# Second attention of a fused network: the order of scores and products inside a round, the product cut in halves, and the order of four PSUM banks

## The chip, the cores and the metric

The program runs on one core of one Trainium2 chip, as one launch. The metric is the device time of the launch in microseconds (us), as the median of several runs; lower is better.

## The reference, cut to what matters

The network has two layers; x has shape (2, 1024, 256) in float32. The change touches only the second attention (`L0_attn_b`), which adds its output to x:

```python
NH, NKV = 16, 4                       # 16 query heads, 4 heads of keys and values
HD = C // NH                          # 16
q = _rope((x @ Wq).reshape(b, t, NH, HD).transpose(0, 2, 1, 3))
k = _rope((x @ Wk).reshape(b, t, NKV, HD).transpose(0, 2, 1, 3))
v = (x @ Wv).reshape(b, t, NKV, HD).transpose(0, 2, 1, 3)
k, v = jnp.repeat(k, 4, axis=1), jnp.repeat(v, 4, axis=1)
scores = jnp.einsum('bhqd,bhkd->bhqk', q, k) / sqrt(HD)
scores = jnp.where(causal, scores, finfo.min)
y = jnp.einsum('bhqk,bhkd->bhqd', jax.nn.softmax(scores, axis=-1), v)
return y.transpose(0, 2, 1, 3).reshape(b, t, c) @ Wproj
```

## The kernel before, in words

All arithmetic is in float32. The stage treats four chunks of 512 query rows, one after the other: batch 0 rows 0 to 511 (c = 0) and 512 to 1023 (c = 1), then batch 1 likewise. Within a chunk it goes through t = 0 to 3; one t stands for four query heads, one for each head g of keys and values, and the four g lie at partitions 32g, so that four matmuls of 32 rows can run side by side in the array.

For each t the scores are computed twice.

- `highest` (L891, matmuls at L898, called Q below) makes scores by query rows: for 128 queries and up to 512 keys, one PSUM bank for each g. VectorE reduces each bank to the negated row maximum (L906 where the diagonal has to be masked, L911 elsewhere) and writes it beside the queries. A list `quads` holds these steps, 16 for a chunk with c = 0 and 32 for a chunk with c = 1, over (t, 128 queries, up to 512 keys). With c = 1 the eight steps of one t have 512, 128, 512, 256, 512, 384, 512 and 512 keys.
- `turn` (L913) transposes the queries of one t with their maxima into `qm` (matmuls at L919, copied out by ScalarE at L921). With c = 1 VectorE first merges two maxima (L916).
- `round_.scores` (L928, matmuls at L933, called S) makes the same scores by keys: 128 keys by m queries, again one bank for each g. ScalarE takes the exponential of each bank into `pr` (L938); GpSimd zeroes what lies above the diagonal (L942).
- `round_.weigh` (L947, matmuls at L952, called W) multiplies `pr` with v into the bank `py`, which is accumulated over the key blocks kb. After the last block `divide_by_sums` (L997) runs on VectorE: a transpose (L1002), a reciprocal (L1004), a product (L1008) and, for every second t, one more transpose (L1013).

With c = 0 the four blocks of a t have m = 512, 384, 256, 128; with c = 1 the eight have 512 five times, then 384, 256, 128. A matmul in float32 leaves two rows in the profile.

Seven PSUM banks (tag "sc") go round in the order in which tiles are asked for; the eighth is `py`. A matmul into a tile waits until the instruction that last read that bank is done.

The order of PE, VectorE, ScalarE and GpSimd is the order of issue in the source (`in_order`). The loop over n at L824 issues one step of `quads`, the first `piece` of the list for this n, W of the round issued two steps earlier, S of the round that lags ten steps behind `quads`, then `turn` where one is due, then the other pieces. Pieces are the work for the next chunk (transposes, projection at L327 with its rope on VectorE, `turn_keys` L882, `turn_queries` L888) and the output products of the chunk before (L965, added to x at L970). They are spread over the first three chunks; the last chunk has only the output pieces of the one before.

Of the kernel before, what the change touches and what calls it, by code (L numbers as in the profile page):

```python
# [27 lines left out]
def interleave(a, b):  # L28

    ia = ib = 0  # L30
    while ia < len(a) or ib < len(b):
        if ib >= len(b) or (ia < len(a) and ia * len(b) <= ib * len(a)):
            a[ia]()
            ia += 1
        else:
            b[ib]()
            ib += 1
# [102 lines left out]
class Net:  # L140
# [625 lines left out]
    def attn_b(self, w, wo, cos, sin, ffn):  # L766

        nc, tc = self.nc, self.tc
        lead = 10
        with ExitStack() as ctx:
            big = ctx.enter_context(tc.tile_pool(name="b_big", bufs=1))
            work = ctx.enter_context(tc.tile_pool(name="b_work", bufs=2))
            ps = ctx.enter_context(tc.tile_pool(name="b_ps", bufs=1, space=PSUM))


            qpad = [big.tile([P, 4, 4, 4, 32], F32, name=f"q_pad{j}") for j in range(2)]
            kpad = [big.tile([P, 4, 32], F32, name=f"k_pad{j}") for j in range(2)]
            for p in qpad + kpad:
                nc.gpsimd.memset(p, 0.0)
            for p in kpad:
                nc.gpsimd.memset(p[:, :, 16:17], 1.0)

            mask = big.tile([P, 512], BF16, name="mask")
            nc.gpsimd.memset(mask[:, 0 : 512 - P], 0.0)  # L790
            nc.gpsimd.tensor_copy(mask[:, 512 - P :], self.neg)
            ctx.enter_context(self.in_order())
            pools = (ps, big, work, w, wo, cos, sin, kpad, mask)
            chunks = []
            for b in range(B):
                kT = big.tile([P, T], F32, tag="kT", name="kT", bufs=2)
                v = big.tile([P, NB, 4, 32], F32, tag="v", name="v", bufs=2)
                nc.gpsimd.memset(v[:, :, :, 16:32], 1.0)
                chunks += [self.attn_b_chunk(pools, b, c, kT, v, qpad[c]) for c in range(2)]

            def bank(name):
                return ps.tile([P, 512], F32, tag="sc", name=name, bufs=7)

            owed = [step for _, step in self.ffn0_pieces(work, bank, 12, *ffn)]
            interleave(owed, chunks[0].inputs)
            quads, rounds, turns, fill = [], [], {}, {}

            def add(n, step):
                fill.setdefault(n, []).append(step)

            for n, chunk in enumerate(chunks):
                at = len(quads)
                size = len(chunk.quads)
                inputs = chunks[n + 1].inputs if n + 1 < len(chunks) else []
                for m, steps in enumerate(self.spread([1.0] * (size - 1), inputs)):
                    for step in steps:
                        add(at + m, step)
                for j, step in enumerate(chunk.outputs):
                    add(at + size + lead + 3 + j, step)
                for t in range(4):  # L820
                    turns[at + (t + 1) * size // 4] = chunk.turns[t]
                quads += chunk.quads
                rounds += chunk.rounds
            for n in range(max(fill) + 1):  # L824
                pieces = fill.get(n, [])
                here, last = (
                    rounds[n - lead - j] if 0 <= n - lead - j < len(rounds) else None
                    for j in (0, 2)
                )
                if n < len(quads):  # L830
                    quads[n]()
                for piece in pieces[:1]:
                    piece()
                if last:
                    last.weigh()
                if here:
                    here.scores()
                if n in turns:
                    turns[n]()
                for piece in pieces[1:]:  # L840
                    piece()

    def attn_b_chunk(self, pools, b, c, kT, v, qk):
# [5 lines left out]
        end = 4 * c + 3  # L849

        def psum(name):
            return ps.tile([P, 512], F32, tag="sc", name=name, bufs=7)
# [38 lines left out]
        def highest(t, j, lo):  # L891

            i = 4 * c + j
            n = min(512, (i + 1) * P - lo)
            tiles = [psum("s1") for _ in range(4)]
            for g in range(4):
                rows = slice(32 * g, 32 * g + 32)
                nc.tensor.matmul(  # L898
                    tiles[g][:, 0:n], shared["qT"][rows, t, j * P : (j + 1) * P],
                    kT[rows, lo : lo + n], start=True, stop=True,  # L900
                )
            for g in range(4):
                out = qk[:, j, t, g, HD : HD + 1] if lo == 0 else shared["nm2"][:, t, j, g : g + 1]
                if lo + n == (i + 1) * P:
                    masked = work.tile([P, 512], F32, tag="masked", name="masked")
                    nc.vector.tensor_tensor_reduce(  # L906
                        masked[:, 0:n], tiles[g][:, 0:n], mask[:, 512 - n :], -1.0, 3e38,
                        ALU.add, ALU.min, out,
                    )
                else:  # L910
                    nc.vector.tensor_reduce(out, tiles[g][:, 0:n], AX.X, ALU.max, negate=True)  # L911
# [11 lines left out]
        def round_(t, kb):  # L923
            own = type("round", (), {})()
            q0 = max(512 * c, kb * P)
            m, off = 512 * (c + 1) - q0, q0 - 512 * c

            def scores():  # L928
                pr = own.pr = work.tile([P, 4, 512], F32, tag="pr", name="pr", bufs=4)
                tiles = [psum("s2") for _ in range(4)]  # L930
                for g in range(4):
                    rows = slice(32 * g, 32 * g + 32)
                    nc.tensor.matmul(  # L933
                        tiles[g][:, 0:m], kT[rows, kb * P : (kb + 1) * P],
                        shared["qm"][t][rows, off:512], start=True, stop=True,
                    )
                for g in range(4):
                    nc.scalar.activation(pr[:, g, off:512], tiles[g][:, 0:m], AF.Exp, scale=0.25)  # L938
                if kb >= 4 * c:

                    d = pr[:, :, off : off + P]
                    nc.gpsimd.affine_select(  # L942
                        out=d, in_=d, compare_op=ALU.is_ge, fill=0.0, base=0,
                        pattern=[[0, 4], [1, P]], channel_multiplier=-1,
                    )

            def weigh():  # L947
                if kb == 0:
                    shared["py"] = ps.tile([P, 512], F32, tag="py", name="py")
                py = shared["py"]  # L950
                for g in range(4):
                    nc.tensor.matmul(  # L952
                        py[32 * g : 32 * g + 32, off:512], v[:, kb, g, :], own.pr[:, g, off:512],
                        start=(kb == 0), stop=(kb == end),
                    )
                if kb == end:
                    self.divide_by_sums(work, py, shared["yT"], t)

            own.scores, own.weigh = scores, weigh
            return own  # L960

        def output(j):
# [9 lines left out]
        chunk = type("chunk", (), {})()  # L972
        chunk.quads = [
            lambda t=t, j=j, lo=lo: highest(t, j, lo)
            for t in range(4) for j in range(4) for lo in range(0, (4 * c + j + 1) * P, 512)
        ]
# [1324 lines left out]
```

## Time and profile before

| What | Value |
|---|---|
| Median of 3 runs | 2863.79 us (2859.41 to 2870.02) |
| Profiled execution: span from first to last instruction | 2865.0 us |
| Mean granted TensorE clock of the core | 0.932 |
| Busy share of the span | PE 88%, PEld 54%, DVE 71%, ACT 46%, POOL 37% |
| Matmul rows at L898, L933, L952 | 768 each |
| First Q, first S, first W, last W (start) | 504.3, 535.1, 541.7 and 873.0 us |

The page gives no time of the profiled execution other than its span, which is 1.2 us above the median of the runs. PE is the matmul engine, PEld its weight loads, DVE VectorE, ACT ScalarE, POOL GpSimd. In a timeline row the columns are the start and the length in us, the engine, the source line, the operation, output and inputs, the shape, how many instructions were merged into the row, and in brackets the idle time of the engine before it and what ended it. Ends of matmuls are modelled; starts are recorded. A group of four matmuls that runs side by side shows as x8.

### The profile page before, as it was taken

The numbers are of one execution on the slowest core, as the hardware profiler recorded it, in microseconds if no ns is written. First come the engines' busy times: TensorE is split into PE (matmuls) and PEld (weight loads), VectorE is DVE, ScalarE is ACT, GpSimd is POOL, SyncE is SP. The second block draws the span as 40 slices with busy tenths as digits, with TensorE's granted clock in tenths as the row PEclk, the third lists the DMA queues.
The fourth block names the chain that finished last, engine by engine and source line by source line (L and its number), as shares of the span: only waits on it lengthen the run. The fifth ranks groups of instructions, "written<-read, shape, count | busy, mean of one in ns | idle before, by whom it ended". The sixth has DMA issues, their size and how long they took to land.

```text
span 2865.0 us, 66910 instructions
## 1 busy us (share of the span) xinstructions
PE 2520.3 (88%) x26384; PEld 1555.7 (54%) x26384; DVE 2028.8 (71%) x6762; ACT 1330.0 (46%) x2800; POOL 1063.2 (37%) x1600
## 2 busy tenths in 40 slices
PE   6999998999998877988888888888868999989888
PEld 2334334444433444655655555555646777767777
DVE  5777774766767968679786878788656767767651
ACT  2686870345454435676666675757611222212110
POOL 3444242211115757567554665565510001101000
PEclk9999998999999966999998999899978999999898
DMA  4000000000001100000000000000011110101100
GB/s 122 1 1 1 1 1 1 1 1 1 1 1 45 45 1 1 1 1 1 1 1 1 1 1 1 1 1 1 1 35 25 25 25 22 21 15 35 25 9 15
DMA packets 61978, 35.37 MB, mean 12 GB/s; under 512 B 43216, under 2 KB 58080, under 8 KB 61664
## 3 DMA queue, kind: packets, MB, share of 16 engines
q1 hardware_dynamic: 59472, 29.49, 4.0%
q8 instruction: 207, 3.39, 0.5%
q10 hardware_dynamic: 2192, 1.61, 0.2%
q14 instruction: 107, 0.88, 0.1%
HBM read 22.68 MB, written 8.39 MB: 11 GB/s over the span
## 4 chain that ended last, share of the span: by engine, by line
PE 38%; DVE 14%; POOL 4%; ACT 4%; issue 3%; SPq 1%; DMA 1%; ACTq 0%; POOLq 0%; DVEq 0%
PE ph L1521 6%; PE pg L2115 5%; PE e L1273 4%; DVE p L1284 4%; PE pu L2115 4%; PE po L2133 3%; PE dT L1345 3%; PE po L1540 2%; DVE p L1323 2%; POOL p L1331 1%; PE py L1375 1%; POOL p L1311 1%; ACT p L1294 1%; PE kh L1726 1%; PE pq L327 1%
## 5 line engine op out<-in xcount | busy, mean ns | idle before, releaser
L1294 ACT ACTIVATE p<-p,nm 128x128 f32<-128x128 f32 (+7 forms) x512 | 391.2, 769 | 79.8 <-DVE nm L1290 42.2
L1284 DVE CUSTOM_DVE_ANT_0 p<-e,mask 128x512 f32<-128x512 f32 (+3 forms) x768 | 382.3, 553 | 61.4 <-PE e L1273 61.0
L1331 POOL TENSOR_SCALAR p<-p,md 128x128 f32<-128x128 f32 (+7 forms) x256 | 241.6, 948 | 180.0 <-DVE md L1323 162.6
L1359 ACT ACTIVATE pT<-dT 128x384 f32<-128x384 f32 (+3 forms) x384 | 176.6, 487 | 203.2 <-PE dT L1345 202.2
L1273 PE MATMUL e<-kT,qT 32*128 32x512 f32 (+3 forms) x1536 | 230.5, 580 | 43.7 <-DVE nm L1284 40.8
L1345 PE MATMUL dT<-ident,p 128*128 128x128 f32 x1152 | 197.1, 297 | 65.2 <-POOL p L1331 36.6
L1323 DVE CUSTOM_DVE_ANT_0 p<-p,nrs 128x128 f32<-128x128 f32 (+7 forms) x256 | 221.3, 890 | 25.9 <-POOL p L1315 25.7
L938 ACT ACTIVATE pr<-s 128x512 f32<-128x512 f32 (+3 forms) x384 | 157.3, 496 | 162.9 <-PE s L933 154.2
L1311 POOL TENSOR_SCALAR p<-p,ra,neg_lam 128x128 f32<-128x128 f32 (+7 forms) x256 | 219.5, 857 | 9.2
L1345 PEld LDWEIGHTS dT<-ident,p 128*128 128x128 f32 x1152 | 138.0, 149 | 153.5 <-POOL p L1331 67.9
L654 ACT ACTIVATE pr<-s 128x1024 f32<-128x1024 f32 (+1 forms) x192 | 145.4, 813 | 125.6 <-PE s L648 77.4
L2115 PE MATMUL pg<-xT,gate 128*128 128x256 f32 x576 | 158.6, 423 | 4.6 <-ACT inter L2120 3.4
L898 PE MATMUL s<-kT,qT 32*128 32x512 f32 (+3 forms) x768 | 155.0, 518 | 4.3 <-DVE q_pad L906 2.5
L906 DVE CUSTOM_DVE_ANT_0 masked<-s,mask 128x128 f32<-128x128 f32 (+3 forms) x256 | 110.7, 487 | 59.1 <-PE s L898 59.0
L659 ACT ACTIVATE pr<-pr 128x1024 f32<-128x1024 f32 (+1 forms) x192 | 152.2, 852 | 0.0
L2133 PE MATMUL po<-down,inter 128*128 128x256 f32 x576 | 144.2, 395 | 5.8 <-DVE inter L2125 5.8
L1273 PEld LDWEIGHTS e<-kT,qT 32*128 32x128 f32 x1536 | 84.8, 203 | 116.3 <-DVE nm L1284 72.7
L662 POOL TENSOR_SCALAR_AFFINE_SELECT pr<-pr 128x256 f32<-128x256 f32 x128 | 89.3, 716 | 152.1 <-ACT pr L659 55.1
L2115 PE MATMUL pu<-xT,up 128*128 128x256 f32 x576 | 141.3, 389 | 0.8 <-ACT inter L2120 0.7
L2120 ACT ACTIVATE inter<-pg 128x512 f32<-128x512 f32 x72 | 43.0, 597 | 195.7 <-PE pg L2115 195.7
L2115 PEld LDWEIGHTS pg<-xT,gate 128*128 128x128 f32 x576 | 116.5, 209 | 27.1 <-issue 4.7
L300 POOL TENSOR_SCALAR ln_xn<-x,ln_mv,rsq_y 128x256 f32<-128x256 f32 x128 | 89.8, 710 | 108.1 <-DVE rsq_y L279 88.8
(295 smaller groups left out, 5344.1 us busy)
## 6 DMA issues: line engine op xcount, KB each, us to landing
uk_d<-uk SPq DMA_DIRECT2D x128, 32.0 KB, 1.9
r<-uk_d SPq DMA_DIRECT2D x8, 512.0 KB, 3.5
x<-in_L_attn_a_X SPq DMA_DIRECT2D x4, 512.0 KB, 6.7
qh_d<-qh SPq DMA_DIRECT2D x8, 256.0 KB, 2.1
o<-qh_d SPq DMA_DIRECT2D x128, 16.0 KB, 1.8
out<-x SPq DMA_DIRECT2D x4, 512.0 KB, 4.4
w<-in_L_ffn_W2T SPq DMA_DIRECT2D x1, 1024.0 KB, 7.7
pk<-in_L_ffn_gate_packed SPq DMA_DIRECT2D x8, 128.0 KB, 2.4
```

Of the source, the lines that this page charges most:

```text
L938: nc.scalar.activation(pr[:, g, off:512], tiles[g][:, 0:m], AF.Exp, scale=0.25)
L1273: nc.tensor.matmul(own.tiles[h][:, a, 0 : hi - lo], made["q"][r : r + 32, a, t, :], kT[r : r + 32, a, lo:hi], start=True, stop=True,)
L1284: nc.vector.tensor_tensor_reduce(own.p[h][a][:, lo:hi], own.tiles[h][:, a, 0 : hi - lo], neg_row[:, T - nk + lo : T - nk + hi], -1.0, 3e38 ...
L1294: nc.scalar.activation(own.p[h][a], own.p[h][a], AF.Exp, bias=own.nm[:, h, a : a + 1], scale=-1.0, accum_out=own.sm[:, h, a : a + 1],)
L1311: nc.gpsimd.tensor_scalar(p1, p1, own.ra[:, h : h + 1], nlam[:, head : head + 1], ALU.mult, ALU.mult)
L1323: nc.vector.tensor_tensor_reduce(p0, p0, p1, own.nrs[:, h : h + 1], 3e38, ALU.add, ALU.min, own.md[:, h : h + 1],)
L1331: nc.gpsimd.tensor_scalar(p0, p0, -1.0, own.md[:, h : h + 1], ALU.mult, ALU.add)
L1345: nc.tensor.transpose(dT[:, n, :], own.p[h][0][:, kb * P : (kb + 1) * P], self.ident)
L1359: nc.scalar.activation(shared[t, s + h][:, lo:hi, :], own.dT[h, part][:, 0 : hi - lo, :], AF.Exp)
L1521: nc.tensor.matmul(ph[:, j, :], w[:, kc, m * P : (m + 1) * P], f.xT[:, kc, :], start=(kc == 0), stop=(kc == 1),)
L2115: nc.tensor.matmul(ph[:, j, :], m_[:, kc, m * P : (m + 1) * P], f.xT[:, kc, :], start=(kc == 0), stop=(kc == 1),)
L2133: nc.tensor.matmul(f.po[:, b], inter[m // 2][:, m % 2, b * P : (b + 1) * P], wd[:, m % 2, (m // 2) * C : (m // 2 + 1) * C], start=(b == m ...
```

## The change

Inside one step n of the loop the order becomes S, the first half of W, Q, the first piece, the second half of W, `turn`, the other pieces. W is cut in the middle of its query columns where it has at least 256 of them (80 of the 96 rounds); a W of 128 columns is issued whole at the place of the first half. The four matmuls of S and of Q are issued from g = 3 down to g = 0, while their banks are still asked for, and read, from g = 0 up.

```diff
+                if here:
+                    here.scores()
+                if last:
+                    last.weigh(0)
                 if n < len(quads):
                     quads[n]()
                 for piece in pieces[:1]:
                     piece()
                 if last:
-                    last.weigh()
-                if here:
-                    here.scores()
+                    last.weigh(1)
                 if n in turns:
                     turns[n]()
...
             tiles = [psum("s1") for _ in range(4)]
-            for g in range(4):
+            for g in reversed(range(4)):
...
                 tiles = [psum("s2") for _ in range(4)]
-                for g in range(4):
+                for g in reversed(range(4)):
...
-            def weigh():
-                if kb == 0:
+            cuts = [off, (off + 512) // 2, 512] if m >= 256 else [off, 512]
+
+            def weigh(part):
+
+                if part + 1 >= len(cuts):
+                    return
+                if kb == part == 0:
                     shared["py"] = ps.tile([P, 512], F32, tag="py", name="py")
                 py = shared["py"]
+                at = slice(*cuts[part : part + 2])
                 for g in range(4):
                     nc.tensor.matmul(
-                        py[32 * g : 32 * g + 32, off:512], v[:, kb, g, :], own.pr[:, g, off:512],
-                        start=(kb == 0), stop=(kb == end),
-                    )
-                if kb == end:
+                        py[32 * g : 32 * g + 32, at], v[:, kb, g, :], own.pr[:, g, at],
+                        start=(kb == part == 0), stop=(kb == end), skip_group_check=True,
+                    )
+                if kb == end and part + 2 == len(cuts):
                     self.divide_by_sums(work, py, shared["yT"], t)
```

## The prediction

> **What bounds the kernel now.** I read the page first, for the groups of the three products, then the windows over the stage, then the timeline of single rounds. Units are us.
>
> ```profile
> L938 ACT ACTIVATE pr<-s 128x512 f32<-128x512 f32 (+3 forms) x384 | 157.3, 496 | 162.9 <-PE s L933 154.2
> ...
> L898 PE MATMUL s<-kT,qT 32*128 32x512 f32 (+3 forms) x768 | 155.0, 518 | 4.3 <-DVE q_pad L906 2.5
> L906 DVE CUSTOM_DVE_ANT_0 masked<-s,mask 128x128 f32<-128x128 f32 (+3 forms) x256 | 110.7, 487 | 59.1 <-PE s L898 59.0
> ```
> ```profile
> 530.00:870.00 340.00, 333.84 (x2426) 142.38 (x2428) 228.24 (x743) 170.71 (x413) 54.82 (x96) 1.00 0.00 1
> ```
> In the window (columns: length, then busy PE, PEld, DVE, ACT, POOL, clock) PE is busy 334 of 340, DVE 228, ACT 171. Exponentials and reductions wait for PE; PE waits for nobody. So the stage is bound by PE's order. But PE is not full, as one round of full width shows:
>
> ```profile
> 814.53 1.07 PE L952 MATMUL py<-pr,v 128*32 128x512 f32 x8
> ...
> 815.53 1.14 PE L933 MATMUL s<-qmT,kT 32*128 32x512 f32 x8
> ...
> 816.49 2.03 PE L898 MATMUL s<-kT,qT 32*128 32x512 f32 x8
> ...
> 816.75 2.06 ACT L938 ACTIVATE pr<-s 128x512 f32<-128x512 f32 x4 [1.64 <-PE s L933]
> 817.39 0.29 PEld L898 LDWEIGHTS s<-kT,qT 32*128 32x128 f32 x2 [0.70 <-ACT pr L938]
> 817.54 2.48 DVE L911 TENSOR_REDUCE q_pad<-s 128x1 f32<-128x512 f32 x4 [1.92 <-PE s L898]
> 818.45 0.16 PEld L952 LDWEIGHTS py<-pr,v 128*32 128x32 f32 x8 [0.76 <-issue]
> ```
> From start to start W takes 1.00, S 0.96 and Q 1.96. Q is twice S because S holds four of the seven banks: three of Q's matmuls go together, the fourth waits for the bank of the first exponential (817.39) and runs alone until 818.45, 1.06. The round is 3.92.
>
> **What the change removes.** With the banks in reverse the first matmul issued waits for the bank that comes free last, and all four then go side by side. Such a group followed by another kind of matmul costs 1.07 (861.86 to 862.93):
>
> ```profile
> 861.86 1.14 PE L933 MATMUL s<-qmT,kT 32*128 32x512 f32 x8
> ...
> 862.93 0.33 PEld L952 LDWEIGHTS py<-pr,v 128*32 128x32 f32 x8 [0.76 <-issue]
> ```
>
> **What it adds on PE.** A half of W is 256 wide and costs 0.57 (the W of 256 columns at 804.49 is followed by S at 805.06), two halves 1.14 instead of 1.00; S, now followed by W, 1.07 instead of 0.96. PE's own work in a full round is 1.07 + 0.57 + 1.07 + 0.57 = 3.28, 0.64 less than now. The 640 further matmul rows (80 split rounds, 8 rows each) lie in these prices.
>
> **What it adds in waits.** Only 7 banks stand against 8 in a round, so each group waits for the one before it.
> - Q waits for S's first exponential. S starts at 815.53, the exponential at 816.75, its bank is free at 817.39: 1.86 (1.81 at 819.44 to 821.25); I take 1.85. PE has S and half of W to do until then, 1.64.
> - The next S needs the bank of Q's first reduction. Q's four end 1.2 after their start, as S's do, a reduction takes 2.48/4 = 0.62 and the release 0.05, together 1.9. PE has Q and half of W, 1.64.
> A full round without a piece becomes 1.85 + 1.9 = 3.75: the 0.64 shrinks to 0.17. Of narrow groups these sums are 1.45, 1.15, 0.85 (S of 384, 256, 128) and 1.55, 1.2, 0.86 (Q), from the same kind of rows; before, narrow rounds simply cost PE less.
>
> Two VectorE steps change places too.
> - **The divide.** W's last block stood behind Q; now its L1002, L1004 and L1008 come ahead of Q's reductions in VectorE's queue, and the next S waits for the first of those:
>
> ```profile
> 808.05 0.72 DVE L1002 STREAM_TRANSPOSE turned<-py 128x512 f32<-128x512 f32 x1
> ...
> 808.80 0.25 DVE L1004 RECIPROCAL rec<-turned 128x16 f32<-128x16 f32 x1
> ...
> 809.09 0.42 DVE L1008 TENSOR_TENSOR pair<-turned,rec 128x256 f32<-128x256 f32 x1
> ```
>  That is 1.46, and 0.71 more for every second t.
> - **The turn.** With c = 1, L916 stands in VectorE's queue behind all four reductions of this step's Q, and PE stands at the transposes behind it:
>
> ```profile
> 824.05 1.86 PE L898 MATMUL s<-kT,qT 32*128 32x512 f32 x8
> ...
> 825.10 2.48 DVE L911 TENSOR_REDUCE q_pad<-s 128x1 f32<-128x512 f32 x4 [1.11 <-PE s L898]
> 825.84 1.06 PE L952 MATMUL py<-pr,v 128*32 128x512 f32 x8
> ...
> 826.83 0.71 PE L933 MATMUL s<-qmT,kT 32*128 32x256 f32 x8
> ...
> 827.50 0.17 DVE L916 TENSOR_TENSOR q_pad<-q_pad,nm 128x16 f32<-128x16 f32 x1
> ...
> 827.73 0.66 PE L919 MATMUL qm_ps<-ident,q_pad 128*128 128x128 f32 x4 [0.19 <-DVE q_pad L916]
> ```
>  From Q to the turn it is 3.68, now covered by Q, W and S. In the new order only Q and half of W are left, 1.64, and Q ends later since all four go together: 1.2 + 2.48 + 0.25 = 3.95, so PE stands still for 2.3. Queued behind it are S and with it ScalarE.
>
> **The sum, one t of eight rounds (c = 1, no pieces).** Key blocks 0 to 7 meet Q of 512, 256, 512, 384, 512, 512, 512, 128 keys. New: 3.75; block 1 has the divide (VectorE busy with the last Q until 1.8, divide to 3.25 or 4.0, first reduction 0.42, so 4.1 on the mean); 3.75; 1.85 + 1.55 = 3.4; 3.75; block 5 waits for the fourth reduction of the Q before at 1.85, then 1.9, 3.75; block 6 with the turn 1.85 + 3.95 + 0.59 = 6.4; block 7 0.85 + 0.86 = 1.7. Together 30.6. Before: 804.49 to 831.43, the starts of W of 256, 26.94. So +3.7 a cycle; its first six rounds alone, 22.5 against 21.15, +1.35.
> - Steps 26 to 47 and 74 to 95 are of this kind, two cycles and six rounds each: 2 x (7.4 + 1.35) = +17.5. Pieces give back. An output piece of 1.06 fills waits: 1.85 + 1.07 + 1.06 + 0.57 = 4.55 against 4.98 now, and beside a turn it is hidden whole; a small one (0.26) takes a bank, so that S waits for one more reduction, +0.36. Over 8 output, 4 projection and some 9 small pieces I count -8. Net +9.5.
> - Steps 16 to 25 and 64 to 73 (Q of c = 1 with S of 512, 384, 256, 128): by the same sums steps 64 to 73 take 4.0, 2.05, 3.75, 4.1, 3.05, 3.35, 3.75, 4.4, 6.4 and 1.7, together 36.5, with two divides and one turn, against 30.5 now (from the Q that starts at 741.25 to the one at 771.74), less 0.7 for one output piece that fills a wait. The short S no longer shorten a round. Some +5 each, +10.
> - Steps 48 to 63 (short Q, a piece in nearly every round): where S has 512 and Q 256 beside a projection, 1.85 + 0.65 + 1.49 + 0.57 = 4.55 against 4.76, where a small piece stands beside a wide Q up to 0.4 more; on the whole -1. Steps 0 to 15 (no W yet, or pieces throughout) and the end without Q: 0, within 3.
> Sum +18.5. On the profiled 2865.0 that is 2883.5; on the median, 1.2 lower, 2882.
>
> Bounds: 0.1 in each of the 84 rounds' waits is 8 either way. The six wide turns are 9 to 14, or nothing if the merge comes sooner. The clock is a risk from above: waits of VectorE already lowered it where Q runs alone, but not in the loose end of the stage.
>
> ```profile
> 510.00:515.00 5.00, 3.84 (x10) 1.72 (x10) 4.62 (x22) 0.00 (x0) 1.47 (x4) 0.50 0.00 0
> ...
> 860.00:876.00 16.00, 12.07 (x108) 3.52 (x105) 2.11 (x4) 10.45 (x26) 2.55 (x4) 1.00 0.01 2
> ```
> The new rounds (3.28 of 3.75 busy, the turn aside) are nearer to the second row, so I price the clock at 0; a half clock of 3.4 at each of 8 turns would be +14 if PE bound it, and twice that for 6.8.
>
> The Trainium skill speaks against such an order: "TensorE: Matmul & The Clock Gate", in "A second HAM failure mode: psum-queue depth-cycling", says that PE waiting briefly between groups as PSUM banks cycle lets the clock swing between half and full. The row at 860, with its waits and a clock of 1.00, does not show it; by the page's figure of half the clock the whole of the 340 would be open to a far larger loss, as an estimate 340/0.75 - 340 = 113 us if it swung half the time with PE as the bound.
>
> **The rivals.**
> - *Faster: PE stays the bound.* If the half products and pieces cover the waits for banks at S and Q, a full round is 3.28. It decides at the next S: if its bank is free 1.64 after Q instead of 1.9. About 50 full Q at 0.64 and the narrow ones for a little: -35, 2829. For it: PE idles 6 of 340 today. Against: it idles so little because single matmuls fill the very waits.
> - *No change: the turn is covered.* The six wide turns stand in the sum with about 1.5 each after what pieces hide, 9, and ten divides beside a Q of c = 1 with 0.9, 9. If S's earlier place lets VectorE run ahead so that both are covered, nothing is left: about 2864. For it: VectorE is busy only 228 of 340. Against: its queue is in order, and the rows above stand behind Q whatever its idle time.
> - *Slower still: the clock.* Holes of 2.3 at the turns drop the clock: +14 to +27 on top, about 2903. For it the row at 510, against it the row at 860, which has holes of up to 1.8.
> - *It does not do what it says.* Q still runs in two pieces, for its banks come free one by one: then only the added 0.36 a split round is left, 80 x 0.36 = +29, 2893.
>
> **How the numbers follow.** A measurement tells about 0.5%, 14 us, from no change. Chances: my sum 0.50 (0.84 of it over 2878), clock 0.14, two pieces 0.08, covered turn 0.18, PE the bound 0.10. Slower 0.42 + 0.14 + 0.08 = 0.64; same 0.08 + 0.18 = 0.26; faster 0.10. The likeliest is my sum, 2882. For 8 in 10 the range leaves out most of the PE rival and the far end of the clock: 2853 to 2910.
>
> **What would show it.** L952 has 1408 rows. Q of 512 runs as one group of four, about 1.07 to the next group. PE's idle time names DVE q_pad L906 and L911 before S, ACT pr L938 before Q, and about 2.3 before L919 behind L916 in six turns. PE's busy time in the stage falls by 30 or more while its span grows. The forecast is wrong if PE stays over 95% busy, if Q still shows a lone matmul, or if the turns wait under 1.

## The result: 1.7% slower, more than twice what was forecast

| | before | after |
|---|---|---|
| Median of the runs, us | 2861.6 (2857.96 to 2870.02) | 2913.76 (2910.82 to 2918.24) |
| Ratio to before, 95% interval | 1 | **1.0173** (1.0152 to 1.0194) |
| Span of the profiled execution, us | 2865.0 | 2909.2 |
| Mean granted TensorE clock of the span | 0.932 | 0.924 |

The direction was right, the size was not: 2882 was forecast, with 2910 as the upper end. In the profiled executions the changed kernel is 44.2 us longer, and the forecast sum was +18.5. All of it arises in the stage of the second attention; the first S starts at 535.3 in the one profile and at 535.1 in the other.

### The profile page after: what moved, and what is told of

It reads as the page before. It is cut to its first block, busy times and chain, and to the rows that moved or that the text cites. A ratio compares the mean times of both kernels' runs of the same rounds, so it can differ in the third digit from the quotient of the medians.

```text
span 2909.2 us, 68108 instructions
## 1 busy us (share of the span) xinstructions
PE 2549.1 (88%) x27024; PEld 1572.3 (54%) x27024; DVE 2028.9 (70%) x6762; ACT 1329.8 (46%) x2800; POOL 1056.9 (36%) x1600
## 4 chain that ended last, share of the span: by engine, by line
PE 37%; DVE 15%; POOL 4%; ACT 4%; issue 3%; SPq 0%; DMA 0%; POOLq 0%; DVEq 0%; ACTq 0%
PE ph L1529 5%; PE pg L2123 4%; PE e L1281 4%; DVE p L1292 4%; PE pu L2123 4%; PE po L2141 3%; PE dT L1353 3%; PE po L1548 2%; DVE p L1331 2%; PE py L1383 1%; POOL p L1339 1%; ACT p L1302 1%; POOL p L1319 1%; PE kh L1734 1%; PE pq L327 1%
## 5 line engine op out<-in xcount | busy, mean ns | idle before, releaser
L944 POOL TENSOR_SCALAR_AFFINE_SELECT pr<-pr 128x512 f32<-128x512 f32 x64 | 41.4, 646 | 252.5 <-ACT pr L940 162.8
L900 PE MATMUL s<-kT,qT 32*128 32x512 f32 (+3 forms) x768 | 130.6, 571 | 1.7 <-DVE q_pad L908 1.5
L2123 PEld LDWEIGHTS pg<-xT,gate 128*128 128x128 f32 x576 | 115.6, 208 | 28.2 <-issue 6.9
```

The costliest lines, as they stand in the source:

```text
L2123: nc.tensor.matmul(ph[:, j, :], m_[:, kc, m * P : (m + 1) * P], f.xT[:, kc, :], start=(kc == 0), stop=(kc == 1),)
```

## The profile after

The same window view as before, now over the longer stage. Its columns are length, busy PE, PEld, DVE, ACT and POOL, then the granted clock.

```profile
530.00:917.00 387.00, 366.58 (x3062) 161.40 (x3060) 231.57 (x759) 172.77 (x416) 54.91 (x97) 0.93 0.01 1
```

Before, the clock of this stage was 1.00 and PE was idle for about 6 us. Now the clock is 0.93 and PE is idle for 20. VectorE and ScalarE are busy for about as long as before (232 and 173 us, then 228 and 171), so no work was added there. The groups of instructions of this stage (busy time, mean ns, idle time ahead of them and what ended it):

```profile
L940 ACT ACTIVATE pr<-s 128x512 f32<-128x512 f32 (+3 forms) x384 | 156.9, 499 | 162.8 <-PE s L935 162.7
L900 PE MATMUL s<-kT,qT 32*128 32x512 f32 (+3 forms) x768 | 130.6, 571 | 1.7 <-DVE q_pad L908 1.5
L935 PE MATMUL s<-qmT,kT 32*128 32x512 f32 (+3 forms) x768 | 124.2, 563 | 7.2 <-DVE nm L908 5.3 <-DVE q_pad L908 1.8
L960 PE MATMUL py<-pr,v 128*32 128x256 f32 (+2 forms) x1408 | 103.2, 372 | 0.4 <-POOL pr L944 0.4
L921 PE MATMUL qm_ps<-ident,q_pad 128*128 128x128 f32 x64 | 11.3, 301 | 13.1 <-DVE q_pad L918 13.1
```

Q (L900) fell from 155.0 to 130.6 us of PE. The last line shows the one large new wait: 13.1 us ahead of the turn's transposes, for the merge of the two maxima. The second and third show that S and Q still wait for almost nothing in the records. That doesn't mean that they run as wanted, as the timeline of a full round shows:

```profile
859.85 1.28 PE L935 MATMUL s<-qmT,kT 32*128 32x512 f32 x8
861.05 0.64 PE L960 MATMUL py<-pr,v 128*32 128x256 f32 x8
861.62 1.37 PE L900 MATMUL s<-kT,qT 32*128 32x512 f32 x8
862.92 0.64 PE L960 MATMUL py<-pr,v 128*32 128x256 f32 x8
863.49 1.19 PE L935 MATMUL s<-qmT,kT 32*128 32x384 f32 x8
```

From start to start S takes 1.20, Q 1.30 and each half of W 0.57, so the round is 3.64 against 3.92 before: the change does shorten a full round. But S and Q take longer than the 1.07 of four matmuls side by side. They start one or two at a time as banks come free, and such a staggered group counts as busy. The turn, some steps later:

```profile
868.72 1.76 PE L900 MATMUL s<-kT,qT 32*128 32x512 f32 x8
870.52 2.48 DVE L913 TENSOR_REDUCE q_pad<-s 128x1 f32<-128x512 f32 x4 [1.21 <-PE s L900]
...
872.92 0.18 DVE L918 TENSOR_TENSOR q_pad<-q_pad,nm 128x16 f32<-128x16 f32 x1
...
873.24 0.63 PE L921 MATMUL qm_ps<-ident,q_pad 128*128 128x128 f32 x4 [2.19 <-DVE q_pad L918]
```

PE stands still for 2.19 until VectorE has worked through the four reductions and the merge. The chain of the prediction is there row by row. Over the eight turns with c = 1 this wait is 0.36 to 2.19 us. What the prediction left out shows in rows and windows of the same run:

```profile
574.27 1.21 PE L935 MATMUL s<-qmT,kT 32*128 32x256 f32 x2 [2.66 <-DVE nm L908]
785.40 1.11 PE L935 MATMUL s<-qmT,kT 32*128 32x256 f32 x2 [0.84 <-DVE nm L908]
```
```profile
572.00:582.00 10.00, 7.73 (x53) 2.69 (x53) 6.45 (x19) 2.00 (x8) 2.27 (x4) 0.66 0.01 2
...
845.00:872.00 27.00, 26.05 (x224) 10.46 (x224) 17.07 (x50) 13.17 (x28) 2.54 (x4) 1.00 0.00 1
```

In the rounds from 845 up to the turn's hole at 871 PE never stands still in the records, and the clock is full. At 574 PE had waited 2.66 us for VectorE (S of 256 keys, behind the divide and the first masked reductions), and the clock was halved for 6.8 us. At 785 a wait of 0.84 at the same place was followed by 10.2 us. There are eight such stretches from the first exponential of S to the last, of 3.4, 6.8 or 10.2 us each, 51.2 us in all. Before there was none.

This gives an account that serves for every run below: the stage from the first exponential of S to the last, its growth over before (335.0 us), PE's further idle time in it, half of the time at half clock (what it would cost if PE bounded throughout), and the rest, which is PE being busy for longer or shorter. It is an account and not a proof, since ends of matmuls are modelled, and half clock during an idle stretch costs nothing. Each row is also one profiled execution. Over the whole span the clock lost (1 less the granted clock, times the span) was 216 to 225 us in the four runs of the changed kernel and 180 to 210 in 23 of the kernel before: the changed kernel's loss is no accident of one execution, but a difference of some 10 us between two rows can be one.

| Run | Ratio | Stage | Idle | Half clock / 2 | Rest |
|---|---|---|---|---|---|
| after | 1.0173 | +46.2 | +14.5 | 51.2 / 2 = 25.6 | +6.1 |
| e1 reversal alone | 1.0079 | +21.9 | +3.1 | 1.7 | +17.1 |
| e2 forward banks | 1.0078 | +29.7 | +13.1 | 22.2 | -5.6 |
| e3 banks fixed | 1.0187 | +52.6 | +58.6 | 22.2 | -28.2 |
| e4 turn early | 1.0084 | +28.3 | +5.8 | 12.0 | +10.5 |
| e5 forward, turn early | 1.0057 | +18.8 | +6.4 | 13.8 | -1.4 |
| e6 as e5, divide late | 1.0083 | +22.9 | +12.6 | 18.8 | -8.5 |
| e7 divide late | 1.0159 | +48.3 | +24.5 | 22.2 | +1.6 |
| e8 turn's wait filled | 1.0105 | +36.0 | +3.2 | 12.0 | +20.8 |
| e9 filled, more | 1.0119 | +37.9 | +1.4 | 5.1 | +31.4 |
| e10 forward, merge early | 1.0024 | +10.6 | +3.4 | 10.3 | -3.1 |
| e11 as e5, W whole | 1.0089 | +28.2 | +13.3 | 15.4 | -0.5 |
| e12 single-file filler | 1.0280 | +66.0 | -1.9 | 30.7 | +37.2 |
| e13 reversed, merge early | 1.0086 | +25.3 | +2.0 | 12.0 | +11.3 |
| e14 before, turn behind Q | 1.0083 | +24.8 | +13.6 | 12.0 | -0.8 |
| e15 before, W in halves | 1.0011 | +1.9 | 0.0 | 1.7 | +0.2 |
| e16 as e10, divide late | 1.0022 | +11.2 | +8.8 | 12.0 | -9.6 |

## The experiments

**The reversal alone (e1)**: the kernel before, `for g in reversed(range(4))` in both places.

> The old order of a round, with only the four matmuls of S and of Q issued from g = 3 down. Theory T1 (the loss lies in the new places of the steps: PE waits at the turn and at the divide, and the clock drops in those holes): no loss here, within 5 us of before. Theory T2 (a bank is given to a tile when its first matmul is issued, not when the tile is asked for; so in the reversed order the matmul that waits longest writes g = 0, which ScalarE and VectorE read first): VectorE starts on Q about 1 us later in each round, the first exponential after a waiting S up to 0.9 later; PE covers much of it with W, so +8 to +35 us; and Q still shows three matmuls and one alone. Theory T3 (the extra switches of the halved product cost PE 0.36 us a round): 0.

Measured 1.0079 (1.0059 to 1.0100). Q of 512 keys takes 2.08 in a full round (842.10 to 844.18) where it took 1.96: it isn't one group of four. Its matmuls start at 842.10, 842.11, 842.30 and, alone, 843.13. If each tile had its bank from the line that asks for four, the first of them would have waited for the last bank; so a tile gets its bank only when its first matmul is issued (e3, where the banks are fixed, is the contrast). The reversal therefore only makes g = 0, which VectorE and ScalarE read first, the last one written: VectorE's first reduction starts 2.19 after Q (844.29), where it started 1.05 after it (817.54).

**The new order with banks forward (e2)**: the changed kernel, `for g in range(4)` in both places.

> The changed kernel with the four matmuls of S and of Q issued from g = 0 up again. T1: the holes at the turns (about 2.3 us at six or seven of them) and the lower clock stay, +30 to +50 us against before. T2: VectorE and ScalarE start on the first bank while the last matmul still waits; a round without turn takes 3.4 to 3.6 us instead of 3.6 to 3.9, so that half or more of the 52 us goes: +0 to +25 us. T3: +25 to +35 us.

Measured 1.0078 (1.0054 to 1.0101). Taking the reversal out of the changed kernel wins about what putting it into the old one lost. The turn's hole gets shorter, but stays (2.30 from the start of W at 856.04 to the transposes, 2.83 in the changed kernel), and so does most of the half clock.

**Banks as the prediction took them (e3)**: seven tags of one bank each, handed out in the order of the requests.

```diff
+            turn_of = itertools.cycle(range(7))
+            self.sc_bank = lambda name: ps.tile(
+                [P, 512], F32, tag=f"sc{next(turn_of)}", name=name, bufs=1
+            )
```

> The changed kernel with the seven banks handed out strictly in the order in which tiles are asked for (seven tags of one bank each), so that the matmul issued first, g = 3, has the bank that comes free last. This is what the prediction took for granted. T1: Q and S run as groups of four, 1.07 us to the next group, and PE waits ahead of them; the time is the predicted sum plus the lower clock, +18 to +45 us. T2: the four no longer wait one by one, a gain on the changed kernel of 5 to 25 us, +25 to +45 us against before. T3: as the changed kernel, +52 us.

Measured 1.0187 (1.0169 to 1.0206), no better than the changed kernel. Timeline of PE in it:

```profile
859.40 1.14 PE L904 MATMUL s<-kT,qT 32*128 32x512 f32 x8 [0.21 <-ACT pr L944]
860.47 0.64 PE L964 MATMUL py<-pr,v 128*32 128x256 f32 x8
861.36 1.14 PE L939 MATMUL s<-qmT,kT 32*128 32x512 f32 x8 [0.24 <-DVE q_pad L917]
862.42 0.64 PE L964 MATMUL py<-pr,v 128*32 128x256 f32 x8
863.27 0.93 PE L904 MATMUL s<-kT,qT 32*128 32x384 f32 x8 [0.21 <-ACT pr L944]
```

This is the round that the prediction describes: groups of four at 1.07, Q waiting for the first exponential, S for the first reduction. The round is 1.07 + 0.89 + 1.07 + 0.84 = 3.87, and 3.75 was forecast for it. PE's own saving is there (-28.2 in the account), and the waits of whole groups eat it twice (+58.6). In plain busy time PE's saving is 6.0 us, since half clock lengthens what is left. Groups of four aren't what the changed kernel does, and they would not have helped it. A window of these rounds, in which single waits of PE go up to 0.87, has the clock full:

```profile
850.00:872.00 22.00, 18.50 (x188) 5.67 (x184) 13.07 (x40) 11.97 (x24) 1.46 (x3) 1.00 0.00 1
```

**The turn ahead of Q (e4)**: `turns[n]()` moved from behind the second half of W to ahead of `quads[n]()`; banks reversed.

> The changed kernel with the turn issued ahead of Q instead of behind the second half of W, so that its merge on VectorE no longer stands behind this step's four reductions. T1: eight merges stop holding PE for 2.2 us, and the clock stays up there: -12 to -30 us against the changed kernel, +22 to +40 us against before. T2: the holes go, but the rounds stay as they are: -8 to -16 us against the changed kernel. T3: no gain, +52 us.

Measured 1.0084 (1.0064 to 1.0105). The turn belongs to the t that is complete before this step's Q, so nothing but the order makes it wait for these reductions. Moving it wins about 0.9%, 25 us in the medians and 17.9 in the profiled stage; there PE's idle time fell by 8.7 and the half clock by 27.3.

**Both, and the divide (e5, e6, e7).** e5 is e4 with banks forward. e6 is e5 with `divide_by_sums` issued behind Q, as before. e7 is the changed kernel with only the divide moved so.

> The changed kernel with matmuls from g = 0 up and the turn ahead of Q. T1 with T2 (the reversal and the place of the turn are two separate losses of about 25 us each): both go, and the time is -5 to +5 us against before. If both were one loss (the same idle time seen twice): +15 to +25 us. T3 (the extra switches of the halved product): +25 us or more.

> As the run before, and the divide on VectorE issued behind Q's reductions again, as in the kernel before, instead of ahead of them. T1: some ten divides stop holding the next S for about 1 us each, a further -5 to -15 us, so -5 to -20 us against before, faster than both kernels. If the divide costs nothing: as the run before. T3: +20 us or more.

> The changed kernel with the divide alone put behind Q's reductions; the reversed order and the late turn stay. T1: -5 to -15 us against the changed kernel, +35 to +47 us against before. If the divide's place costs nothing: +52 us.

Measured 1.0057 (1.0038 to 1.0077), 1.0083 (1.0058 to 1.0108) and 1.0159 (1.0123 to 1.0195). Against their partners (1.0057 for e6, 1.0173 for e7) the divide's place gains nothing that can be told. e5 lies where one loss seen twice was expected (16 us over before): with the whole turn ahead of Q the reversal costs 0.27 percent (e4 less e5), and 0.95 with the late turn. Where its cost went, e16 shows below.

**A filled hole (e8, e9)**: e8 puts 12 repeated transposes of the identity ahead of the four real ones of a turn with c = 1, into the same bank, so that PE works while it waits; no wait is taken away. e9 also repeats three of S's matmuls, side by side, in the third key block.

```diff
+            for j in range(12 if c == 1 else 0):
+                nc.tensor.transpose(pt[:, j % 4, :], self.ident, self.ident)
```

> The changed kernel with twelve further transposes of the constant identity into the turn's own bank ahead of the four real ones, in the eight turns of c = 1 that wait for the merge; they fill some 1.6 us of the 2.2 us in which PE stands. The hole in the order stays, only the clock can gain. If the clock falls because of these holes and costs time: the half clock of 55 us in the stage falls under 25 and the time by 8 to 20 us. If the clock follows the general waiting or costs nothing: the time stays within 4 us of the changed kernel.

> The kernel with the filled turns, and in S of key block 2, where the last matmul waits for the bank behind the divide, the three matmuls of g = 3, 2, 1 issued again (three times over with c = 0, once with c = 1) with the same operands into the same banks; they change no value. If the half clock is what the prediction missed, at about 0.5 us for each us of it: the 27 us left with the filled turns fall under 15, and the time falls by 3 to 10 us more, to +20 to +28 us against before, which is the predicted sum of waits (+18.5). If the clock costs nothing: no gain, or a loss of up to 10 us from the added matmuls.

e8 measured 1.0105 (1.0079 to 1.0131): added work made the changed kernel 0.7% faster. Half clock fell from 51.2 to 23.9 us. Its four runs lost 200 to 211 us of clock over the span, where the changed kernel lost 216 to 225. So the clock isn't a by-product of the waits, it is a cost beside them. e9 measured 1.0119 (1.0099 to 1.0138), a miss. In its profiled stage half clock fell on to 10.2 us, but PE's own time rose by 10.6 over e8 (31.4 against 20.8 in the last column); and over the span its four runs lost 203 to 218, no less than e8's, so that a further gain in clock is not shown.

**Only the merge ahead of Q (e10)**: e2, with L916's merge of two maxima issued ahead of Q and the transposes left late.

```diff
+                if n in turns:
+                    turns[n][0]()          # the merge
                 if n < len(quads):
                     quads[n]()
...
-                    turns[n]()
+                    turns[n][1]()          # the transposes
```

> The changed kernel with matmuls from g = 0 up, only the merge on VectorE (L916 of before) issued ahead of Q, and the transposes left behind the second half of W. If the wait of the transposes for VectorE is what the turn costs: it falls from 2.2 us, and from 0.7 us with the whole turn ahead of Q, to nearly 0, and the time is 4 to 10 us below the run with the turn ahead of Q, +5 to +14 us against before. If the transposes wait for all of Q's reductions anyway (same tile): as the run with forward matmuls alone, +20 to +25 us.

Measured 1.0024 (1.0004 to 1.0044), the best of the new orders with e16, and still no faster than before. One VectorE instruction of 0.18 us, moved ahead of the reductions it doesn't need, is worth 15 us there.

**W whole in the new order (e11)**: e5 with `cuts = [off, 512]`.

> The order alone: S, the whole of W, Q, piece, with matmuls from g = 0 up and the turn ahead of Q; W is not cut in halves. T3 (the switches of the halved product cost 0.36 us a round): faster than the same order with halves, by 10 to 25 us. T1 (the halves fill waits on both sides): a full round is Q 1.1 to 1.3, then 0.7 or more of waiting for the first reduction, about 3.7 to 3.9 us instead of 3.4; slower than with halves by 5 to 20 us, +20 to +37 us against before.

Measured 1.0089 (1.0074 to 1.0104) against 1.0057 for e5: the halves are a small help, not a cost.

**Single-file filler (e12)**: e10, and in the third key block one of S's matmuls is repeated nine times (c = 0) or three times (c = 1) into its own bank.

> As the run with the merge ahead of Q, and S of key block 2 filled by repeating the matmul of g = 2 (nine times with c = 0, three times with c = 1). If the clock is the rest of the loss: half clock under 15 us and -5 to +5 us against before, the best of all orders. If not: +5 to +20 us.

Measured 1.0280 (1.0260 to 1.0299), the opposite of what it was for. Timeline row and windows of e12:

```profile
558.56 5.75 PE L940 MATMUL s<-qmT,kT 32*128 32x256 f32 x26
```
```profile
558.60:564.20 5.60, 5.60 (x31) 4.30 (x25) 3.01 (x10) 1.09 (x4) 0.63 (x1) 0.88 0.02 4
564.20:570.60 6.40, 6.40 (x50) 2.48 (x52) 3.21 (x7) 1.77 (x7) 0.63 (x1) 0.57 0.00 0
```

PE is busy for all of 558.6 to 570.6, and yet the clock is halved from 562.9 on for 6.8 us. All ten stretches of half clock in the stage of e12 begin in a step that holds these repeats (S of the third key block). The repeats use 32 of the array's 128 rows, one after the other. So an idle PE isn't needed to lose the clock; a few us of matmuls in single file in a quarter of the array were enough. Eight of the ten stretches have no hole above 0.3 us in the 4 us before them; the other two follow holes of 1.45 and 2.01.

**What was left open then.** The early merge had only been run with forward banks, and half clock, but for one stretch of 3.4 us in e1, only been seen in the new order.

> The changed kernel with one thing moved: in steps with a turn the merge of the two maxima is issued ahead of Q instead of behind the second half of W; the transposes stay late and the banks reversed. If the late merge and the reversal are separate losses (forward banks alone took the ratio from 1.017 to 1.008, forward banks with the early merge to 1.002), this stands at 1.017 - 0.006 = about 1.011, with PE's 2.2 before the turn's transposes gone and half clock below 30 us. If the two are one loss (the turn only hurts because reversed groups end late), it stands at 1.002 to 1.006 like the forward one. If the merge matters only with forward banks, it stays at 1.015 or more.

e13 (the changed kernel with e10's edit) measured 1.0086 (1.0062 to 1.0110). With e2 and e10 this makes a square:

| Ratio | merge behind Q and W | merge ahead of Q |
|---|---|---|
| banks reversed | 1.0173 (after) | 1.0086 (e13) |
| banks forward | 1.0078 (e2) | 1.0024 (e10) |

Reversal costs 0.95 or 0.62, the late merge 0.87 or 0.54 percent; the remaining 0.33 would be a cost of both together, but intervals of 0.2 percent on each of the four can't tell it from nothing. The stage's waits for the merge are gone in e13 (0.4 in one wait, 13.1 in eight in the changed kernel):

```profile
PE qm_ps L925 <- DVE q_pad L920: 0.4, 1, 0.4
```

e14 is the kernel before with the turn issued right behind Q: the old order and banks, and holes that nothing covers.

> The kernel before, its order and banks as they were, with only the turn moved to the place right behind Q, ahead of the piece, W and S, so that the transposes wait for the merge behind Q's four reductions with nothing to cover them. Per turn of c = 1, by the rows of before: Q to merge end 3.68, of which Q itself covers 2, so a hole of 1.7; at c = 0 the transposes wait for nothing new. If holes cost only themselves: 8 x 1.7 = +14 us, 1.005, clock 1.00 in the stage but for a little. If a hole in an otherwise full order also drops the clock, as I now think: some 10 to 30 us of half clock and +25 to +35, 1.009 to 1.012.

Measured 1.0083 (1.0061 to 1.0106). Its wait, and its window over the stage:

```profile
PE qm_ps L919 <- DVE q_pad L916: 14.1, 7, 3.2
```
```profile
530.00:900.00 370.00, 349.14 (x2456) 150.85 (x2459) 232.00 (x755) 174.32 (x422) 55.30 (x98) 0.97 0.00 1
```

PE's idle time grew by 13.6, and the stage by 24.8. Half of the 23.9 us of half clock is 12.0, and 13.6 + 12.0 = 25.6. A hole in this stage costs nearly twice its length, in an order that was otherwise untouched. This is the account's clearest case, since nothing else was changed. Its six runs lost 199 to 217 us of clock over the span, the profiled one the least, so 12.0 is no high figure.

> The kernel before with each W of at least 256 columns issued as two halves back to back; order and banks as before. The prediction's prices give +0.14 for each of 80 split rounds where PE bounds, so +11 us, 1.004. If halving is free because weight loads hide behind the matmuls, 1.000. If the further 640 matmul rows cost PE their issue, over 1.008.

e15 measured 1.0011 (0.9996 to 1.0026), no difference that can be measured. Two halves back to back take 1.00 in the timeline, as one whole W does.

> The changed kernel with forward banks, the merge ahead of Q, and the divide behind Q's reductions in VectorE's queue: the best of the new orders so far (1.0024) and the divide's wait taken away (there S of the second key block runs in eight separate matmuls over 2.99 us). If that wait is a loss of its own, 10 times some 1.2 us: 0.998, the only version that would beat the kernel before. If, as with the late turn, the wait only moves to the next W, which needs py: 1.002 to 1.004.

e16 measured 1.0022 (1.0008 to 1.0035), as e10 did. The wait view of e16 says where the divide's cost went:

```profile
PE py L965 <- DVE turned L1017: 13.2, 10, 1.9
```

S hardly waits behind the divide any more (1.0 us in two waits); instead the next t's first W waits for the bank `py` that the divide reads, 13.2 us in ten waits. The wait is the same one at another door.

## Why the prediction was wrong, step by step

- **"I price the clock at 0": this is the step that failed, the term of the sum that was mis-sized.** The stage has 51.2 us at half clock, worth 25.6 if PE bounds. The forecast sum was +18.5; with 25.6 it would be 44.1, and the stage grew by 46.2. The row at 860 was the wrong witness: its waits are 1.11, 0.89 and 1.78 us (before 868.21, 872.02 and 875.65), and the holes of the new order, behind the turn and the divide, are up to 2.66. That evenly loose rounds keep the clock was right as far as it went: in e3 the window from 850 to 872 has PE busy for 18.50 of 22 us at a clock of 1.00. The rival that put the clock on top, 2903, was nearest, with its mechanism shown by e8 and e14; it had the holes at the turns only. The larger part sits around steps 16 to 25 and 64 to 73, where short score groups, the divide and the turns meet: of the 51.2 us at half clock the stretches at 573.9, 594.4 and 785.5 alone hold 27.2 us.
- **"The first matmul waits for the last bank, and all four then go side by side": wrong.** That was the rival "it does not do what it says", which had 0.08. Groups start staggered, and reversal costs PE time of its own: +17.1 of PE in e1, and 11.7 in the last column from e2 to the changed kernel. e3 shows that the step's consequences were worked out nearly right (a round of 3.87 for 3.75) for a kernel that this was not.
- **The waits' sum held, by luck.** Without the clock the stage grew by 46.2 - 25.6 = 20.6, for +18.5. But it is made up of other terms: PE was to save time and wait for more, and instead it waited for 14.5 and saved nothing. e3, the kernel that the sum was worked out for, grew by 52.6 - 22.2 = 30.4 without the clock. The first seven rounds of a t without half clock took 3.40, 2.86, 4.63, 3.57, 3.64, 3.71 and 6.60 (S starts 845.39 to 873.80), 28.4 together; 3.75, 4.1, 3.75, 3.4, 3.75, 3.75 and 6.4 were forecast, 28.9. The divide's cost arrives one round later. Two starting figures of the sum are not in the rows: the six rounds put at 21.15 take 21.35 (804.49 to 825.84), which takes 0.4 off the sum, and no Q starts at 741.25; the one meant starts at 740.19, and the ten steps take the 30.5 of the sum only less a piece of 1.06.
- **The turn: right.** 2.3 was forecast; the six wide turns waited for 1.50 to 2.19 each, 11.1 together where 9 to 14 was forecast, and all eight for 13.1. e4 and e13 show it removable by order alone.
- **The divide: visible, but not a price.** Ten waits were put at some 0.9 each. Moving it back gains nothing (e6, e7), since the same VectorE work then holds up `py` (e16).
- **The halves: priced right, credited too little.** 80 times 0.14 was charged, 11 us. With another kind of matmul between them two halves do take 2 x 0.57, as the timeline above shows; back to back they take 1.00, and e15, which runs them so, grew by 1.9 in the stage. Yet the new order is 0.3 percent slower without them (e11 against e5), so they fill more time than they cost.
- **"PE's busy time falls by 30 or more": wrong.** It rose by 31.7, because staggered groups and half clock both count as busy.
- The Trainium skill's "TensorE: Matmul & The Clock Gate", in "A second HAM failure mode: psum-queue depth-cycling", lets the clock swing where PE idles briefly and often between groups. The clock did swing here, for 51.2 us, but not in such rounds: the evenly loose ones of e3 kept 1.00. The estimate of 113 us that the prediction drew from the page assumed swinging half the time; the clock was halved in 13% of the stage.

What stays open: what exactly trips the clock. In the changed kernel seven of the eight stretches begin during or within 2.3 us after a hole of 1.45 to 2.66 us, the eighth after a wait of 0.84; two holes of 1.50 were followed by none. In e14 holes of 3.18 and, three times, 1.92 were followed by one, holes of 2.62 and 1.92 were not, and the stretch at 708.4 has no hole ahead of it. Single-file matmuls with PE never idle did it too (e12), so that idle time need not be the trigger even where there is some: staggered groups stand beside many of these holes, and no run parts the two. The account's last column also isn't split further in the runs with several edits.

No version ran faster than the kernel before; e10 and e16 come within 0.25%.

## What to carry to other kernels

Where PE bounds a stage at full clock, holes of about 2 us may cost about twice their length (e14: 13.6 us of holes, 24.8 of time), though not each of them does; and look for one cheap instruction that stands in an in-order queue behind work that it doesn't need: moving the 0.18 us merge won 0.5 to 0.9%. Before counting on which buffer a group waits for, find out whether a tile is bound to its bank at the request or at the first write; the starts of the single matmuls show it. A wait moved to another consumer of the same slow chain (the divide: from S to W) isn't a gain.

## What the runs showed that was not expected

- The granted clock fell to half for 3.4, 6.8, 10.2 or once (e11) 17.1 us, multiples of 3.4 in every run, in the stage mostly within 4 us after a hole of PE, of 0.5 to 3.6 us, but also without one (e14 at 708.4, eight times in e12); in e14 the holes cost about as much again in clock (13.6 idle, 12.0 clock).
- Useless work can pay: 12 repeated transposes in a hole made the changed kernel 0.7% faster (e8). Useless work of the wrong shape doesn't: single-file matmuls over 32 rows of the array dropped the clock with PE busy throughout (e12, all ten stretches), while e9's repeats side by side went with the least half clock of the new orders in a profiled stage, 10.2 us.
- Four matmuls of 32 rows side by side save PE time over staggered ones (by the account 28 us in e3), but waiting to start them together cost twice that (58.6).
